# Counting layer 1's softmax sums once a group: pair sums chained by accumulating DMAs in a two-layer graph attention kernel

## The chip, the cores and the metric

The kernel runs on one core of one Trainium2 chip. A core has a matrix engine (TensorE, PE in the profile; its weight loads are the row PEld), VectorE (DVE), ScalarE (ACT), GpSimd (POOL), and SyncE (SP), which here only issues DMAs. Matmuls read SBUF and write PSUM. Each engine runs its own instructions in order and waits on semaphores for the others. The metric is the device time of one execution in microseconds; smaller is better.

## The reference

Sixteen graphs of 1024 nodes with 256 features go through two layers. Each layer normalizes, applies ReLU, runs masked multi-head attention and adds the result to x:

```python
h = maximum(layernorm(x), 0)
q, k, v = h @ Wq, h @ Wk, h @ Wv            # layer 0: 4 heads of 64; layer 1: 8 heads of 32
s = where(adj allows, q @ k.T * scale, -inf)  # per head, 1024 x 1024
out = softmax(s) @ v                        # softmax over the keys
x = x + out @ Wo + bo
```

All of it is in float32. The softmax needs, for every query and head, the sum of the exponentials over all keys.

## The kernel before, in words

**Groups and steps.** Scores are held transposed: keys on the partitions, 512 queries along the free axis. For each batch, layer, half of the queries (qh) and half of the features (g) there is a `Group`: four heads in layer 1, two in layer 0. So there are four groups a layer and batch. A group runs in steps; a step handles four blocks of 128 keys x 512 queries. A layer-1 group has 8 steps (all four heads, one block of keys each), a layer-0 group has 4 (two heads, two blocks of keys each).

**A step.** `scores` issues four matmuls into two PSUM pairs (L372). `exponentials` applies the mask on VectorE with one scalar_tensor_tensor for each half of the step (L388), from PSUM into an SBUF tile p of 128 x 2048 floats, and takes the exponential on ScalarE in place (L393). `weigh` multiplies p with the values and adds into one PSUM bank, po (L405). Three PSUM pairs (`ps_s`) serve the scores and also the projections; po and pz have one bank each.

**The sums.** The sum over keys on the partitions is a matmul with ones (`count`, L278, into pz), four matmuls a count. In layer 1, GpSimd first adds the p tiles of two steps (`count_steps`, L502, 128 x 2048), so there are four counts a group. In layer 0, `add_tiles` adds within a step and along the group on VectorE and GpSimd (L416, L418) and counts once a group.

**The end of a group.** The unnormalized output is copied out of PSUM (L288), the sum is copied (`spread`, L296) and written through DRAM into a compact shape, inverted on VectorE (`invert`, L305), broadcast back through DRAM by DMAs on SP (tile inv), and multiplied in by GpSimd (`normalize`, L324, tile cat). `test` compares the sums with two bounds on GpSimd (L318, L319). After two groups `end_half` multiplies with Wo (L353) and adds to x on VectorE (L358).

**The order.** `Stream.run` walks all steps of all layers: the layer-0 steps of batch b+1 (16, the first of them called `first[b+1]` or a) stand before the layer-1 steps of batch b (32, from `second[b]` or c). At step i it issues scores(i), then the weighing of step i - 2 (LEAD is 2), then the counts that are due, exponentials(i), and the other work that `later` has put down for step i: statistics and norms (`stats`, `norm`, then `add_bias` on GpSimd, L190), transposes of the normalized rows (`turn`, L200), projections (`k`, `q`, L212; `values`, L241), `end_half`, the mask's loads (L126, issued by GpSimd), DMA transposes (`flip`, L130, issued by SP), conversions (`put`, L136, ScalarE) and second passes for layer 1 (`second`, L144, VectorE). At an even step with one of `k`, `q`, `values`, `end_half` the weighing is put off, and the next step weighs two steps at once. The very last group has `hurry`: its last two steps are counted directly, and it ends with `finish`.

**Buffers.** p tiles alternate between tag p0 (even steps, three buffers) and p1 (odd steps, two).

## Time and profile before

| | us |
|---|---|
| median of 3 runs | 3377.39 (3377.24 to 3378.44) |
| the profiled execution | 3380.06 |
| its span, first to last instruction | 3378.3 |
| TensorE (PE) busy | 3339.0 |
| VectorE (DVE) busy | 2501.1 |
| GpSimd (POOL) busy | 2447.1 |
| ScalarE (ACT) busy | 2182.5 |

The granted TensorE clock was 0.998 of full speed. In a row of the groups by line stand the line, engine and operation, what is written and read, the shapes, the number of instructions, then busy time and mean duration in ns, then the idle time of the engine just before them and what ended most of it. In a timeline a row gives the start, the length, the engine, line, operation and the number of instructions merged. In the waits a row gives who waited for whom, the total, the number and the longest. A float32 matmul appears as two instructions in the records, so a count of four matmuls is eight of them.

### The profile page before, as it was taken

Reading aid. Unit: us, or ns where it says so; the run is one execution under the profiler, and the core shown is the slowest. Engines: PE = TensorE matmul, PEld = TensorE weight load, DVE = VectorE, ACT = ScalarE, POOL = GpSimd, SP = SyncE. Lnnn points to the kernel's source line nnn. Section 1 sums busy time; section 2 is a strip of 40 time slices with the busy share of each in tenths; the row PEclk is TensorE's granted clock in tenths of the full one; section 3 lists DMA queues with packets and bytes.
Section 4 is the critical chain, followed back from the end, with each engine's and each line's share of the span. In section 5 each row is a group of like instructions: output and inputs, shape, how many; then the busy total and the mean of one; then the engine's idle time right before and its main releaser. Section 6 shows DMA issues by size and latency. Waiting matters only on the chain. (4 is left out here: it accounts for less than half of the span.)

```text
span 3378.3 us, 46298 instructions
## 1 busy us (share of the span) xinstructions
PE 3339.0 (99%) x18190; PEld 1298.6 (38%) x18190; DVE 2501.1 (74%) x2664; ACT 2182.5 (65%) x2402; POOL 2447.1 (72%) x1606
## 2 busy tenths in 40 slices
PE   8999999999999999999999999999999999999998
PEld 3443333333333333333334333333343333433432
DVE  4676767767677786777867778677786777777876
ACT  5567566675666756667566675666756667665665
POOL 5577778777677766877677686777867778676776
PEclk9999999999999999999999999999999999999999
DMA  6221111212112111121221212212121111210001
GB/s 131 48 42 36 48 39 36 51 36 47 36 36 51 42 42 36 39 48 42 45 39 36 48 39 48 39 39 45 39 47 37 48 39 36 51 38 18 14 17 31
DMA packets 250738, 141.77 MB, mean 42 GB/s; under 512 B 182416, under 2 KB 217488, under 8 KB 250512
## 3 DMA queue, kind: packets, MB, share of 16 engines
q1 hardware_dynamic: 232080, 105.18, 12.6%
q0 software_dynamic: 18432, 33.56, 6.3%
q8 instruction: 144, 2.36, 0.3%
q14 instruction: 82, 0.67, 0.1%
HBM read 120.33 MB, written 18.34 MB: 41 GB/s over the span
## 5 line engine op out<-in xcount | busy, mean ns | idle before, releaser
L393 ACT ACTIVATE p<-p 128x1024 f32<-128x1024 f32 x1536 | 1615.1, 1057 | 973.8 <-DVE p L388 931.7
L388 DVE SCALAR_TENSOR_TENSOR p<-mask,ps 128x1024 f32<-128x1024 fp8e4 x1536 | 1797.0, 1215 | 583.5 <-PE ps L372 553.8
L502 POOL TENSOR_TENSOR p<-p,p 128x2048 f32<-128x2048 f32 x255 | 1161.9, 4557 | 372.2 <-PE po L405 368.3
L372 PE MATMUL ps<-qT,kT 32*128 32x512 f32 (+1 forms) x6144 | 1145.6, 631 | 7.6 <-DVE p L388 4.9
L405 PE MATMUL po<-p,v 128*32 128x512 f32 (+1 forms) x6144 | 992.4, 601 | 0.4 <-ACT o L288 0.4
L418 POOL TENSOR_TENSOR t<-t,t 128x1024 f32<-128x1024 f32 x192 | 486.2, 2532 | 389.8 <-DVE t L416 341.6
L372 PEld LDWEIGHTS ps<-qT,kT 32*128 32x128 f32 (+1 forms) x6144 | 367.7, 184 | 675.7 <-issue 305.3
L405 PEld LDWEIGHTS po<-p,v 128*32 128x32 f32 (+1 forms) x6144 | 227.8, 118 | 689.4 <-issue 529.1
L416 DVE TENSOR_TENSOR t<-p 128x1024 f32<-128x1024 f32 x192 | 325.0, 1693 | 14.6 <-POOL t L418 14.4
L278 PE MATMUL pz<-p,ones 128*32 128x512 f32 x2056 | 267.8, 593 | 0.2 <-POOL p L502 0.2
L212 PE MATMUL pq<-hT,wk 128*128 128x512 f32 x512 | 240.7, 613 | 3.1 <-ACT hT L201 3.1
L353 PE MATMUL py<-wo,cat 128*128 128x256 f32 x1008 | 237.8, 387 | 4.7 <-POOL cat L324 2.8
L241 PE MATMUL pv<-wv,hT 128*128 128x256 f32 x1024 | 237.9, 385 | 0.1
L212 PE MATMUL pq<-hT,wq 128*128 128x512 f32 x512 | 236.6, 605 | 0.0
L241 PEld LDWEIGHTS pv<-wv,hT 128*128 128x128 f32 x1024 | 189.4, 190 | 71.7 <-issue 24.0
L353 PEld LDWEIGHTS py<-wo,cat 128*128 128x128 f32 x1008 | 185.4, 190 | 80.0 <-issue 33.4
L324 POOL TENSOR_TENSOR cat<-o,inv 128x512 f32<-128x512 f32 x127 | 164.5, 1296 | 10.3 <-DMA inv<-vd 9.3
L416 POOL TENSOR_TENSOR t<-p 128x1024 f32<-128x1024 f32 x64 | 165.0, 2578 | 2.8 <-ACT p L393 2.4
L358 DVE TENSOR_TENSOR x<-py,x 128x1024 f32<-128x1024 f32 x63 | 76.4, 1213 | 118.4 <-PE py L353 118.4
L190 POOL TENSOR_TENSOR x<-x,bo 128x1024 f32<-128x1024 f32 x64 | 152.6, 2385 | 1.5 <-DMA bo<-in_bo_dram 1.4
L212 PEld LDWEIGHTS pq<-hT,wk 128*128 128x128 f32 x512 | 93.5, 192 | 145.2 <-issue 120.1
L212 PEld LDWEIGHTS pq<-hT,wq 128*128 128x128 f32 x512 | 92.2, 189 | 139.8 <-issue 138.3
(51 smaller groups left out, 1635.4 us busy)
## 6 DMA issues: line engine op xcount, KB each, us to landing
adj<-in_adj_dram POOLq DMA_DIRECT2D x128, 256.0 KB, 3.6
x<-in_x_dram SPq DMA_DIRECT2D x32, 512.0 KB
inv<-vd SPq DMA_DIRECT2D x128, 128.0 KB
inv<-vd SPq DMA_DIRECT2D x252, 64.0 KB
out_dram<-x SPq DMA_DIRECT2D x31, 512.0 KB
adjT<-adj SPq DMA_TRANSPOSE x128
sd<-s SPq DMA_DIRECT2D x64, 4.0 KB
sn<-sd SPq DMA_DIRECT2D x64, 4.0 KB
```

The costliest lines, as they stand in the source:

```text
L212: nc.tensor.matmul(pq[:, m, :], wt[self.layer][:, c, ts(m, P)], self.hT[half][:, c, :], start=(c == 0), stop=(c == 1),)
L241: nc.tensor.matmul(pv[:, i, :], self.hT[half][:, c, ts(i, P)], w.v[self.layer][:, c, :], start=(c == 0), stop=(c == 1),)
L278: nc.tensor.matmul(self.s[r * self.D : (r + 1) * self.D, :], w.ones[:, : self.D], p[:, r, :], start=start, stop=stop,)
L324: nc.gpsimd.tensor_mul(self.half.cat[:, self.g, :], self.ob, self.inv)
L353: nc.tensor.matmul(py[:, i, :], self.half.cat[:, c, ts(i, P)], w.o[self.layer][:, c, :], start=(c == 0), stop=(c == 1),)
L372: nc.tensor.matmul(st.ps[i // 2][:, i % 2, :], gr.inp.kT[r * D : (r + 1) * D, gr.g, ts(kt, P)], gr.inp.qT[r * D : (r + 1) * D, gr.g, ts(gr ...
L388: nc.vector.scalar_tensor_tensor(out=half, in0=gr.mask.m[:, kt, ts(gr.qh, 512)].unsqueeze(1).to_broadcast([P, 2, 512]), scalar=BIG, in1=st ...
L393: nc.scalar.activation(half, half, AF.Exp, scale=gr.scale)
L405: nc.tensor.matmul(gr.o[r * D : (r + 1) * D, :], gr.inp.v[:, kt, h * D : (h + 1) * D], st.p[:, i, :], start=(kt == 0), stop=(kt == NT - 1),)
L416: engine.tensor_add(t, st.p[:, 0:2, :], st.p[:, 2:4, :])
L418: nc.gpsimd.tensor_add(t, t, gr.t)
L502: nc.gpsimd.tensor_add(one, one, st.p)
```

## The change

Layer 1: the pair sums of a group are no longer counted one by one. They are added to one another by DMAs that accumulate into the destination in SBUF (`accumulate`, issued by GpSimd): pair 0 into pair 1, that into pair 2, that into pair 3, and then the last sum is counted once, eight steps after it was weighed. Groups marked `brief` (the last group of each batch, the last two of the program) accumulate only pair 0 into pair 1 and count three times; the `hurry` group counts as before. The end of a layer-1 group moves from 2, 4, 7 and 9 steps after its last weighing to 8, 10, 12 and 15 (brief: 2, 4, 6, 9), that of a layer-0 group from 2, 3, 5, 7 to 4, 5, 7, 9.

Layer 0: `add_tiles` works on two steps at a time, in place in the p tiles, so the tag t goes. The bias add becomes an accumulating DMA issued by GpSimd. Two small operations of `stats` and the two of `test` move to VectorE. p0 gets seven buffers, adj, adjT and hn one, most small tiles two; q and the mask are kept in halves. The start loads four adjacency tiles at once into p tiles, and the positions of most other work in the order change: two of the large items a batch (an `end_half`, a `values`, a `q` and projections of the next batch move by some steps) now lie in layer 0, 7 there and 9 in layer 1, where it was 5 and 11; the second mask pass moves from layer 0 into layer 1.

```diff
+        def second(self, u):
+            m = self.m[u // 4][:, ts(u % 4, 2), :]
...
-                nc.gpsimd.tensor_scalar_add(ve, mv[:, :, 1], EPS)
+                nc.vector.tensor_scalar_add(ve, mv[:, :, 1], EPS)
...
-                nc.gpsimd.tensor_scalar_mul(less, mv[:, :, 0], -1.0)
+                nc.vector.tensor_scalar_mul(less, mv[:, :, 0], -1.0)
...
-            nc.gpsimd.tensor_add(
-                rows, rows, w.bo[self.layer].unsqueeze(1).to_broadcast([P, 4, E])
+            nc.gpsimd.dma_start(
+                rows, w.bo[self.layer].unsqueeze(1).to_broadcast([P, 4, E]), accum_op=ALU.add
             )
...
+            self.brief = self.last
...
-                ok = small.tile([P, self.n_f], F32, tag="ok", name=f"ok_{self.n}_{op.name}")
-                nc.gpsimd.tensor_scalar(ok, self.sn, bound, 1.0, op0=op, op1=ALU.mult)
-                nc.gpsimd.tensor_mul(c, c, ok)
+                nc.vector.scalar_tensor_tensor(
+                    out=c, in0=self.sn, scalar=bound, in1=c, op0=op, op1=ALU.mult
+                )
...
-        st.p = pp.tile([P, 4, 512], F32, tag=f"p{odd}", bufs=2 if odd else 3, name=f"p_{st.n}")
+        st.p = pp.tile([P, 4, 512], F32, tag=f"p{odd}", bufs=2 if odd else 7, name=f"p_{st.n}")
...
+    def add_tiles(one, two):
+        a, b = one.p[:, 0:2, :], one.p[:, 2:4, :]
+        nc.vector.tensor_add(a, a, b)
+        engine = nc.vector if one.j else nc.gpsimd
+        engine.tensor_add(b, two.p[:, 0:2, :], two.p[:, 2:4, :])
+        nc.gpsimd.tensor_add(a, a, b)
+        if one.j:
+            nc.gpsimd.tensor_add(a, a, one.gr.t)
+        one.gr.t = a
...
+        def accumulate(self, one, two):
+            nc.gpsimd.dma_start(one, two, accum_op=ALU.add)
...
-            else:
+            elif j % 2:
                 one = self.steps[i - LEAD - 1].p
+                if not gr.brief and j == 7:
+                    self.accumulate(gr.two, gr.one)
                 nc.gpsimd.tensor_add(one, one, st.p)
-                self.later(i + 2, gr.count, one, st.j == 1, st.last)
+                if gr.hurry:
+                    self.later(i + 2, gr.count, one, j == 1, False)
+                elif j == 1:
+                    gr.one = one
+                elif j == 3:
+                    self.accumulate(one, gr.one)
+                    gr.one = one
+                    if gr.brief:
+                        self.later(i + 6, gr.count, one, True, False)
+                elif gr.brief:
+                    self.later(i + (4 if j == 5 else 2), gr.count, one, False, st.last)
+                elif j == 5:
+                    gr.two = one
+                else:
+                    self.later(i + 3, self.accumulate, one, gr.two)
+                    self.later(i + 8, gr.count, one, True, True)
...
-                self.later(i + 2, gr.count_added)
-                at = 2, 3, 5, 7
+                self.later(i + 4, gr.count_added)
+                at = 4, 5, 7, 9
             else:
-                at = (2, 3, 4, 8) if gr.last else (2, 4, 7, 9)
+                at = (2, 4, 6, 9) if gr.brief else (8, 10, 12, 15)
...
+    for st in steps[-2 * NT :]:
+        st.gr.brief = True
...
-            norms(mine, 0, a - 10, a - 9, a - 7, a - 6)
-            half_inputs(mine, 0, a - 5, a + 2, a + 4, a + 6)
-            norms(mine, 1, a - 8, a - 7, a - 5, a - 4)
-            half_inputs(mine, 1, a - 3, a + 8, c + 6, c + 4)
-        for kt in range(NT):
-            later(a + 4 + kt, masks[b].second, kt)
+            norms(mine, 0, a - 15, a - 14, a - 12, a - 11)
+            half_inputs(mine, 0, a - 9, a + 2, a + 4, a + 6)
+            norms(mine, 1, a - 11, a - 10, a - 8, a - 7)
+            half_inputs(mine, 1, a - 3, a + 8, c, a + 12)
+        for i, u in zip((2, 4, 8, 10, 12, 16, 20, 26), range(NT)):
+            later(c + i, masks[b + 1].second, u)
...
+                half_inputs(other, 0, c + 1, c + 4, c + 8, c + 12)
+            norms(other, 1, c + 1, c + 2, c + 3, c + 5)
+            half_inputs(other, 1, c + (13 if b == 0 else 7), c + 16, c + 20, c + 26)
+            for i, t in zip((7, 12, 17, 22, 33, 37, 41, 45), range(NT)):
+                later(a + i - 5 + (t > 4), mask.load, t)
+                later(a + i - 2, mask.flip, t)
+                later(a + i, mask.put, t)
```

## The prediction

> **What bounds the kernel now.** I read busy shares and groups by line first, then TensorE's and VectorE's timelines, then waits.
>
> ```profile
> PE 3339.0 (99%) x18190; PEld 1298.6 (38%) x18190; DVE 2501.1 (74%) x2664; ACT 2182.5 (65%) x2402; POOL 2447.1 (72%) x1606
> L502 POOL TENSOR_TENSOR p<-p,p 128x2048 f32<-128x2048 f32 x255 | 1161.9, 4557 | 372.2 <-PE po L405 368.3
> L278 PE MATMUL pz<-p,ones 128*32 128x512 f32 x2056 | 267.8, 593 | 0.2 <-POOL p L502 0.2
> L190 POOL TENSOR_TENSOR x<-x,bo 128x1024 f32<-128x1024 f32 x64 | 152.6, 2385 | 1.5 <-DMA bo<-in_bo_dram 1.4
> adj<-in_adj_dram POOLq DMA_DIRECT2D x128, 256.0 KB, 3.6
> ```
>
> PE reads 99% at granted clock 0.998: matmuls taken off it should shorten the span. The timeline qualifies that (start, length):
>
> ```profile
> 1558.12 1.04 PE L278 MATMUL pz<-p,ones 128*32 128x512 f32 x8
> 1559.09 1.14 PE L372 MATMUL ps<-qT,kT 32*128 32x512 f32 x8
> 1560.17 1.06 PE L405 MATMUL po<-p,v 128*32 128x512 f32 x8
> 1561.16 1.51 PE L372 MATMUL ps<-qT,kT 32*128 32x512 f32 x8
> 1562.61 1.06 PE L405 MATMUL po<-p,v 128*32 128x512 f32 x8
> 1563.49 1.04 PE L278 MATMUL pz<-p,ones 128*32 128x512 f32 x8
> ```
>
> A count (L278) stands 0.97 us before the next scores; a weighing followed by scores has the same 0.10 switch, so a count is worth **0.87**. From starts: layer-1 scores 1.07, weighing 0.99, two together 1.84, a large item (k, q, values, end_half) 3.65, a turn 1.02. The 1.51 is not work: the second scores of a pair wait 0.37 for a PSUM pair. I call a pair of steps heavy with a large item, light without. A light layer-1 pair takes 5.36: 4.12 work, 0.87 count, 0.37 wait. In such pairs VectorE shows
>
> ```profile
> 3257.23 4.62 DVE L388 SCALAR_TENSOR_TENSOR p<-mask,ps 128x1024 f32<-128x1024 fp8e4 x4 [0.75 <-PE ps L372]
> 3262.59 4.62 DVE L388 SCALAR_TENSOR_TENSOR p<-mask,ps 128x1024 f32<-128x1024 fp8e4 x4 [0.74 <-PE ps L372]
> ```
>
> so it idles only 0.75 in 5.36, and GpSimd needs 4.56 for its pair sum (L502). Without the count, light pairs belong to VectorE and GpSimd; only heavy pairs (7.63 of PE work) keep the whole 0.87. The waits already name the next limit:
>
> ```profile
> DVE p L388 <- POOL p L502: 27.6, 16, 2.1
> ```
>
> The 7.6 us of idle that the page gives for L372 hides the stalls inside a row.
>
> **The change, part by part.** *Counts.* Before, 63 layer-1 groups count four times and the last five: 257. After, 47 count once, 16 (the last group of each batch, and the one before the last) three times, the last five times: 100. Off PE: 157 x 0.87 = **-136.6 us**, ten a batch (8.7). By the busy row (99%) all of it would come off the span; by the rows of 1.51 only where VectorE keeps up. The Trainium skill (Perfetto Trace Analysis, Identifying the Most-Contended Engine) speaks against the first reading: matmul busy share is no measure of TensorE's headroom, the weight loads' share (38% here) is nearer.
>
> *Steady batch.* Layer 0 first scores at 344.55 and 3053.43, 13 batches: 208.4 each. PE work before: 8 layer-0 pairs, 5 heavy (11.05) and 3 light (7.56), 77.9; 16 layer-1 pairs, 11 heavy and 5 light, 104.5; 20 counts 17.4, 4 turns 4.1: 204.0, so 4.4 of waits, 2.4 in light pairs (with 0.48 just after one), 2.0 around layer changes. After: 7 heavy and 1 light, 9 heavy and 7 light, 10 counts, 4 turns: 195.2. So two large items move from layer 1, where they gave VectorE time, into layer 0, which is full of PE work already.
>
> *Waits after, in the seven light layer-1 pairs*, by step from the layer's first (c). I follow VectorE in its order: four L388 at 1.16 start 1.18 after the first scores, and a scores' end comes 1.15 after the L388 that frees its PSUM pair (both as at 1559 to 1564). In a bare pair the third L388 ends 1.18 + 3 x 1.16 = 4.66 after the pair's start, so the next pair's scores end at 5.81 where PE alone would have 4.12 + 1.07 = 5.19: 0.62 lost, at c+14. c+6 and c+28 have a turn (1.02 of PE work) as cover: 0.37 and 0.30. c+18 has two stats with aggregates between its L388 (1.08 in the timeline), and behind them ve and less, now on VectorE, 0.15 each by L166 (182 ns, partly overlapped): 0.62 + 1.38 = 2.0. c+22 has the same 1.38 and a turn, and starts late by 0.8 from the stats of c+21: 1.8. c+24: 0.25. c+30: 0.33, the old wait. Sum 5.7.
>
> *GpSimd.* It loses the bias adds (152.6), four test operations a group (136.7) and ve and less (39.2); those go to VectorE, 256 operations at about 0.2 (L305, 219 ns) = 51 us at most, under heavy pairs but for the pieces counted above. It gains 157 accumulating DMAs (10 a batch) and 64 bias DMAs. The issue price is not shown: the nearest row, L126, is 0.62 for 2 KB written a partition; these write 8 and 4 KB. Per row it stays 0.62, by bytes it is 2.47. I take 0.7, the rows being as many. Busy time falls by 328.5 and rises by 221 x 0.7 = 155, to 2270, yet its order matters. From the start of c+18: the sum of pair 18 can start when its even tile is weighed (12.9) and ends at 17.4; the accumulate (0.7), a load (0.6) and cat (1.29) end at 20.0; the rstd pair (1.04 + 0.22) waits for the stats of c+22 anyway and ends near 21.3; the bias issue near 22.0; so the sum of pair 20 ends at 26.5. VectorE wants to write that pair's odd p tile again at 24.3, for c+25: odd tiles still have two buffers, the seven are for even ones. PE would see 1.6 of the 2.2 (its next large item covers the rest); between 0 and 1.6 I take 0.7, since GpSimd's start times are the least sure. Queued behind in GpSimd are the load of c+25, then its transpose on SP and ScalarE's put at c+29, with some 4 us to spare.
>
> *Accumulation time.* 1 MB is 64 KB an engine. Adjacency loads land in 3.6 with 512 KB read; their DMA share gives 6.3% x 3378 / 128 = 1.7 of transfer, so some 2 fixed. One pass at that rate is 3.4, three (read, read, write) 10: 5 to 12 us. Two pair sums (9.1) always stand between the second and third accumulate, about 8 us between the first and second of the third group, and the count comes five steps (over 11 us) after the third; were it late, every matmul behind it would wait, PE being in order. So waits of 0 to 4 us a batch; I take none, since the lower half fits. The Trainium skill (DMA: Bandwidth & Descriptors, Anatomy of one DMA) has about 2 us plus bytes at 436 GB/s: an estimate of 4.4 for 1 MB, under my lower bound, by which the second rival below falls away; no row here shows an accumulate.
>
> *The rest.* q and mask in halves change addresses, not instructions: 0. hn with one buffer: the norm of the next half (c+24) comes after the turn of the first (c+23): 0. Layer-0 sums are four GpSimd and three VectorE adds a group as before, under layer-0 pairs of 11. The second mask pass (0.85) moves from layer 0 into heavy layer-1 pairs, hidden under a 3.65 item, otherwise 0.85 x 8 a batch. Loads and transposes at single buffers are two steps apart or more. The four early loads remove 21.5 us of GpSimd waits (L126 behind adjT) at the start, off the path: 0, between -5 and +3.
>
> *Sum.* Waits after: 5.7 + 0.7 + 2.0 = 8.4 against 4.4. A steady batch gains 8.7 - 4.0 = 4.7 (208.4 to 203.7); 13 give 61. Layer 1 of batch 0: 4.7. Of batch 14, nine light pairs: 4.5. Of batch 15, seven counts (6.1), but group 2 needs on GpSimd 4 x 4.56 + 1.29 + 3 x 0.7 = 21.6 where its four light pairs took 21.4: 4. An end_half falls into the tail, +0.9, beside the last exponentials. Together -61 - 4.7 - 4.5 - 4 + 0.9 = -73. The profiled execution took 3380.1 around a span of 3378.3; the median of the runs is 3377.4, so 3378.3 - 73 = 3305 in the span is **3304** in the runs.
>
> **Rivals.**
> *All of it arrives* (0.16): light pairs shrink as heavy ones do, because work queued on VectorE drains in the heavy pairs: 3377.4 - 137 = 3241. For: VectorE idles 553.8 us for scores. Against: those idle times lie in heavy pairs.
> *Transfers late* (0.14): at 12 us an accumulate, GpSimd stands at the second and third of a group with all pair sums behind it, 3 us more a batch: 3304 + 14 x 3 = 3346.
> *The issue price makes GpSimd the bound* (0.16, slower). In layer 1 it holds 16 sums 72.9, five cat 6.5, three rstd pairs 3.8, five loads 3.1 and 14 issues: 86.3 + 14 Z. Layer 0 now takes 90.6 (84.9 and 6 counts 5.2, with 0.5 waits), so the batch passes 208.4 when layer 1 passes 117.8: Z = 2.25. By bytes (2.47) it is 120.9, 211.5 a batch, +3.1 x 14 = +43: 3420. For: L126's 0.62 may go with bytes. Against: its rows are as many.
> *Counts not fewer* is excluded by the code, but shown by L278.
>
> **How the numbers follow.** Forecast 0.51, alone 3265 to 3345; 0.03 falls within 0.2% (7 us, about what a measurement here can tell). Faster 0.51 + 0.16 + 0.14 = 0.81, same 0.03, slower 0.16. The range 3239 to 3362 takes in the first rival's value and the transfers' bound, not the issue price's.
>
> **What would show it.** L278 p x800 instead of 2056; heavy pairs of 7.63; light ones 4.7 to 7, with scores (L372) lengthened beyond 1.14; waits of L388 for the pair sum well over 27.6 us; accumulate issues near 0.7 and landings under 9. Wrong if layer-1 light pairs run at 4.2, if an issue takes over 2 us, or if GpSimd waits for accumulates.

## The result: 8.2% slower

| | us |
|---|---|
| median of the runs after | 3649.97 (3648.04 to 3665.37) |
| median of the runs before, same chip | 3377.38 (3377.24 to 3378.44) |
| ratio, 95% interval | 1.0816 (1.0787 to 1.0846) |
| profiled execution after, its span | 3650.56, 3648.8 |
| granted TensorE clock after (before) | 0.963 (0.998) |

The busy shares of the page, the groups by line, and the accumulates among the DMA issues (median us to landing last). In these rows L402 is the masked copy, L407 the exponential, L386 the scores, L419 the weighing, L520 the pair sum, L506 the accumulate, L198 the bias DMA, L319 the reciprocal of the inversion, L338 normalize; in some runs a number is off by two. Below, `L319 <- sn` stands for that row of the waits.

```profile
PE 3438.5 (94%) x16934; PEld 1322.2 (36%) x16934; DVE 2721.4 (75%) x3048; ACT 2166.1 (59%) x2402; POOL 2307.4 (63%) x1123
```

```profile
L520 POOL TENSOR_TENSOR p<-p,p 128x2048 f32<-128x2048 f32 x255 | 1194.5, 4688 | 272.3 <-PE po L419 224.0 <-ACT hn L190 24.0 <-ACT p L407 10.4
L331 DVE SCALAR_TENSOR_TENSOR chk<-sn,chk 128x8 f32<-128x8 f32 (+1 forms) x256 | 228.7, 893 | 4.4
L151 DVE TENSOR_SCALAR mask<-mask 128x1024 fp8e4<-128x1024 fp8e4 x128 | 165.6, 1294 | 0.0
L292 PE MATMUL pz<-p,ones 128*32 128x512 f32 (+1 forms) x1056 | 164.8, 595 | 0.0
L506 POOL DMA_DIRECT2D p<-p x157 | 144.9, 923 | 69.3 <-PE po L419 39.0 <-POOL p L520 21.4 <-issue 6.1
L198 POOL DMA_DIRECT2D x<-bo x64 | 92.4, 1453 | 16.4 <-ACT hn L190 9.7 <-DMA bo<-in_bo_dram 5.3 <-issue 0.5
```

```profile
p<-p POOLq DMA_DIRECT2D x157, 1024.0 KB, 7.8
```

The counts did go: L292 has 800 instructions for layer 1 and the unchanged 256 for layer 0. Yet TensorE is busy for 100 us more, with 1256 fewer instructions. Two VectorE groups that the prediction took for small are not: L331 (the test) holds 228.7 us at a mean of 893 ns, though its median is 174, and L151 (second mask pass) 1294 ns where it took 850. The waits:

```profile
DVE vn L319 <- DMA sn<-sd: 162.6, 76, 16.7
POOL cat L338 <- DMA inv<-vd: 160.9, 40, 9.6
ACT o L302 <- POOL cat L338: 124.4, 18, 9.0
ACT mask L143 <- DMA adjT<-adj: 41.2, 13, 14.5
```

Before, the first was 43.5, the second 9.3, and the other two are not in the answer. GpSimd itself hardly waits for an accumulate (0.7 us in all). Where does this fall? I took the start of every step's first masked copy (L402) from the trace. Between layer changes a steady batch now takes 89.4 us in layer 0 (before 84.4) and **135.6 in layer 1 (before 123.7)**; the prediction had 90.6 for layer 0, which leaves 113.1 of its 203.7 for layer 1. In layer 0, TensorE idles 0.3 of the 89.4: it simply holds more work there. Layer 1 holds less work and takes longer. From the start of batch 2 to the start of the last layer, that is 230 of the 270 us between the spans; 22 lie before and 18 after. Two stretches show how. A test beside a pair sum:

```profile
1038.15 4.80 POOL L520 TENSOR_TENSOR p<-p,p 128x2048 f32<-128x2048 f32 x1
1038.19 5.01 DVE L331 SCALAR_TENSOR_TENSOR chk<-sn,chk 128x16 f32<-128x16 f32 x2
...
1043.13 1.22 DVE L402 SCALAR_TENSOR_TENSOR p<-mask,ps 128x1024 f32<-128x1024 fp8e4 x1
```

A test of 128x16 numbers lasts until GpSimd's 4.80 us are over, and the next L402 stands behind it. Of the 256 test instructions, 71 last over 1.5 us (175.9 us together), and all 71 end with a GpSimd tensor_tensor. The second stretch begins with a wait for a pair sum and goes on to one for the sums:

```profile
1913.13 4.62 DVE L402 SCALAR_TENSOR_TENSOR p<-mask,ps 128x1024 f32<-128x1024 fp8e4 x4 [3.90 <-POOL p L520]
...
1924.30 1.13 PE L386 MATMUL ps<-qT,kT 32*128 32x512 f32 x4
...
1926.56 0.25 DVE L319 RECIPROCAL vn<-sn 128x16 f32<-128x16 f32 x1 [3.78 <-DMA sn<-sd]
1926.73 2.29 DVE L402 SCALAR_TENSOR_TENSOR p<-mask,ps 128x1024 f32<-128x1024 fp8e4 x2
...
1927.95 2.08 PE L386 MATMUL ps<-qT,kT 32*128 32x512 f32 x4 [2.53 <-DVE p L402]
...
1929.95 1.94 PE L419 MATMUL po<-p,v 128*32 128x512 f32 x8
```

At c+25 VectorE waits 3.90 us for the odd p tile. At c+27 it stands 3.78 us at the reciprocal because its input is still under way through DRAM; the L402 of the next scores is behind it in order, so TensorE waits 2.53. Then the scores take 2.08 where the same four took 1.13, and a weighing 1.94 instead of 1.06. The windows before, in and after the gap (PEclk is the column behind POOL) say why:

```profile
1907.00:1922.00 15.00, 13.53 (x84) 5.30 (x84) 10.13 (x9) 12.27 (x16) 14.08 (x9) 1.00 1.05 181
1926.00:1934.00 8.00, 6.05 (x24) 2.55 (x26) 7.32 (x7) 3.23 (x4) 6.23 (x3) 0.57 0.94 186
1934.00:1944.00 10.00, 8.87 (x52) 3.74 (x51) 6.97 (x6) 9.08 (x9) 3.42 (x2) 1.00 0.51 105
```

The 0.57 is a mean over the window: the trace's records of the granted clock read 1.0 up to 1926.86, 0.5 from there to 1933.68, and 1.0 again. So this stall costs its own 2.53 us and, TensorE being busy for most of the 6.83 us at half the clock, by estimate some 3 more; a longer "busy" TensorE is in part the slow clock.

### The profile page after: what moved, and what is told of

It reads as the page before. It is cut to its first block, busy times and chain, and to the rows that moved or that the text cites. A ratio compares the mean times of both kernels' runs of the same rounds, so it can differ in the third digit from the quotient of the medians.

```text
span 3648.8 us, 44272 instructions
## 1 busy us (share of the span) xinstructions
PE 3438.5 (94%) x16934; PEld 1322.2 (36%) x16934; DVE 2721.4 (75%) x3048; ACT 2166.1 (59%) x2402; POOL 2307.4 (63%) x1123
## 4 chain that ended last, share of the span: by engine, by line
PE 59%; DVE 16%; DMA 11%; ACT 7%; issue 4%; POOL 3%; SPq 1%; DVEq 0%; POOLq 0%; ACTq 0%
PE ps L386 20%; PE po L419 15%; PE pq L225 11%; DVE p L402 9%; PE py L367 5%; PE pv L253 4%; PE pz L292 3%; ACT p L407 3%; DMA sn<-sd 3%; DMA sd<-s 3%; DMA adjT<-adj 2%; DVE chk L331 2%; DMA inv<-vd 1%; POOL p L520 1%; DVE st L173 1%
## 5 line engine op out<-in xcount | busy, mean ns | idle before, releaser
L407 ACT ACTIVATE p<-p 128x1024 f32<-128x1024 f32 x1536 | 1608.9, 1057 | 1082.3 <-DVE p L402 1044.1
L402 DVE SCALAR_TENSOR_TENSOR p<-mask,ps 128x1024 f32<-128x1024 fp8e4 x1536 | 1796.4, 1214 | 581.0 <-PE ps L386 531.4
L386 PE MATMUL ps<-qT,kT 32*128 32x512 f32 (+1 forms) x6144 | 1312.0, 654 | 145.6 <-DVE p L402 104.3
L520 POOL TENSOR_TENSOR p<-p,p 128x2048 f32<-128x2048 f32 x255 | 1194.5, 4688 | 272.3 <-PE po L419 224.0
L419 PE MATMUL po<-p,v 128*32 128x512 f32 (+1 forms) x6144 | 1020.8, 622 | 1.2 <-ACT o L302 1.2
L386 PEld LDWEIGHTS ps<-qT,kT 32*128 32x128 f32 (+1 forms) x6144 | 411.4, 189 | 930.4 <-issue 367.2
L432 POOL TENSOR_TENSOR p<-p 128x1024 f32<-128x1024 f32 x128 | 303.3, 2369 | 344.8 <-DVE p L431 339.8
L419 PEld LDWEIGHTS po<-p,v 128*32 128x32 f32 (+1 forms) x6144 | 230.4, 119 | 716.5 <-issue 501.6
L431 POOL TENSOR_TENSOR p<-p 128x1024 f32<-128x1024 f32 x64 | 151.3, 2364 | 337.2 <-DVE p L428 98.7
L338 POOL TENSOR_TENSOR cat<-o,inv 128x512 f32<-128x512 f32 x127 | 173.9, 1369 | 166.0 <-DMA inv<-vd 160.9
L331 DVE SCALAR_TENSOR_TENSOR chk<-sn,chk 128x8 f32<-128x8 f32 (+1 forms) x256 | 228.7, 893 | 4.4
L302 ACT COPY o<-po 128x512 f32<-128x512 f32 x128 | 74.1, 579 | 213.0 <-POOL cat L338 124.4
L506 POOL DMA_DIRECT2D p<-p x157 | 144.9, 923 | 69.3 <-PE po L419 39.0
L143 ACT ACTIVATE mask<-adjT,mhalf 128x1024 fp8e4<-128x1024 bf16 x128 | 145.6, 1139 | 41.2 <-DMA adjT<-adj 41.2
L428 DVE TENSOR_TENSOR p<-p 128x1024 f32<-128x1024 f32 x128 | 166.6, 1301 | 0.0
L151 DVE TENSOR_SCALAR mask<-mask 128x1024 fp8e4<-128x1024 fp8e4 x128 | 165.6, 1294 | 0.0
```

Of the source, the lines that this page charges most:

```text
L331: nc.vector.scalar_tensor_tensor(out=c, in0=self.sn, scalar=bound, in1=c, op0=op, op1=ALU.mult)
L338: nc.gpsimd.tensor_mul(self.half.cat[:, self.g, :], self.ob, self.inv)
L386: nc.tensor.matmul(st.ps[i // 2][:, i % 2, :], gr.inp.kT[r * D : (r + 1) * D, gr.g, ts(kt, P)], gr.inp.qT[gr.qh][r * D : (r + 1) * D, gr.g ...
L402: nc.vector.scalar_tensor_tensor(out=half, in0=gr.mask.m[gr.qh][:, kt, :].unsqueeze(1).to_broadcast([P, 2, 512]), scalar=BIG, in1=st.ps[i] ...
L407: nc.scalar.activation(half, half, AF.Exp, scale=gr.scale)
L419: nc.tensor.matmul(gr.o[r * D : (r + 1) * D, :], gr.inp.v[:, kt, h * D : (h + 1) * D], st.p[:, i, :], start=(kt == 0), stop=(kt == NT - 1),)
```

## The experiments

The theories. **A**: the accumulates' megabytes delay other transfers (sums, inv, adjT), and the engines that work in order stand at them. **B**: GpSimd's pair sums hold VectorE in the small operations that were moved there (the test, and `ve` and `less`, the two of `stats`) and in the second mask pass. **C**: copies wait for one of o's two buffers. **D**: the new places of the inputs' work. All ratios are to the kernel before; L0 and L1 are the mean us of a steady batch in the two layers, taken as above.

| run | us | ratio (95%) | clock | L0 | L1 |
|---|---|---|---|---|---|
| before | 3377 | 1 | 0.998 | 84.4 | 123.7 |
| the change | 3650 | 1.0816 (1.0787-1.0846) | 0.963 | 89.4 | 135.6 |
| no_acc | 3553 | 1.0527 (1.0510-1.0545) | 0.978 | 89.2 | 129.2 |
| acc_small | 3604 | 1.0674 (1.0656-1.0692) | 0.967 | 89.3 | 132.5 |
| test_second | 3633 | 1.0772 (1.0747-1.0797) | 0.963 | 89.9 | 134.8 |
| cat2 | 3629 | 1.0748 (1.0727-1.0768) | 0.967 | 89.2 | 134.6 |
| nochain | 3700 | 1.0960 (1.0942-1.0979) | 0.975 | 84.3 | 142.0 |
| old_sched | 3749 | 1.1099 (1.1081-1.1118) | 0.950 | 89.2 | 143.0 |
| all | 3502 | 1.0379 (1.0361-1.0396) | 0.982 | 88.2 | 126.5 |
| cand | 3595 | 1.0645 (1.0621-1.0670) | 0.963 | 86.5 | 135.5 |
| all2 | 3679 | 1.0894 (1.0876-1.0912) | 0.963 | 88.9 | 136.9 |
| all3 | 3695 | 1.0940 (1.0915-1.0964) | 0.960 | 91.0 | 136.5 |
| b_small | 3668 | 1.0861 (1.0843-1.0880) | 0.968 | 85.6 | 140.1 |
| b_bias | 3373 | 0.9986 (0.9977-0.9996) | 0.997 | 83.4 | 123.7 |
| gps | 3563 | 1.0550 (1.0532-1.0567) | 0.970 | 88.7 | 131.2 |
| gps_no_acc | 3494 | 1.0343 (1.0326-1.0360) | 0.979 | 88.8 | 127.4 |
| all4 | 3486 | 1.0324 (1.0307-1.0342) | 0.980 | 89.0 | 124.7 |
| best | 3605 | 1.0671 (1.0643-1.0699) | 0.961 | 94.4 | 127.7 |
| best_no_acc | 3349 | 0.9908 (0.9891-0.9924) | 0.994 | 88.3 | 116.7 |
| best_small | 3387 | 1.0022 (1.0012-1.0031) | 0.989 | 88.3 | 118.9 |

### One cause at a time, taken from the change

**no_acc.**

```diff
         def accumulate(self, one, two):
-            nc.gpsimd.dma_start(one, two, accum_op=ALU.add)
+            return
...
-            nc.scalar.copy(s, self.s)
+            nc.scalar.activation(s, self.s, AF.Identity, bias=w.ones[:, 0:1])
```

> The changed kernel without its 157 accumulating DMAs; each count then sees one pair of a group alone, and 1 is added to the sums when they are copied so that they stay above zero. Theory A (the accumulates' transfers lengthen the round trip of the sums through DRAM, and VectorE, which takes its work in order, stands at the reciprocal L319, GpSimd at cat L338): the wait L319 <- sn falls from 162.6 us to near the 43.5 of before, cat <- inv from 160.9 to near 9, and the time falls by 120 to 220 us, to 3430 to 3530. Theory B (VectorE is held by GpSimd's pair sums in the test L331 and the second mask pass L151): those two keep their 228.7 and 165.6 us, and the time falls by at most what the 144.9 us of issues give GpSimd, under 60 us, to 3590 to 3650.

**acc_small.** With the same second edit:

```diff
-            nc.gpsimd.dma_start(one, two, accum_op=ALU.add)
+            nc.gpsimd.dma_start(one[:, 0, 0:32], two[:, 0, 0:32], accum_op=ALU.add)
```

> The 157 accumulates stay where they are, with the same number of rows, but each row carries 32 of its 2048 numbers (128 bytes of 8192); 1 is added to the sums when they are copied. It separates the bytes moved from the issue (0.92 us each on GpSimd) and from the waits that the chain needs. Theory A: as without accumulates but for the issues, 3440 to 3560. If the issue and the chain's order on GpSimd cost the time, it stays above 3590. Theory B: above 3590 as well.

**test_second.**

```diff
-                nc.vector.scalar_tensor_tensor(
-                    out=c, in0=self.sn, scalar=bound, in1=c, op0=op, op1=ALU.mult
-                )
+                ok = small.tile([P, self.n_f], F32, tag="ok", name=f"ok_{self.n}_{op.name}")
+                nc.gpsimd.tensor_scalar(ok, self.sn, bound, 1.0, op0=op, op1=ALU.mult)
+                nc.gpsimd.tensor_mul(c, c, ok)
...
-        for i, u in zip((2, 4, 8, 10, 12, 16, 20, 26), range(NT)):
-            later(c + i, masks[b + 1].second, u)
+        for u in range(NT):
+            later(a + 4 + u, masks[b].second, u)
...
```

> The changed kernel with the test back on GpSimd as four small operations, and the second mask pass back in layer 0 of the next batch; accumulates as in the change. Theory B: VectorE gets back some 184 us held in the test and 77 in the mask pass, GpSimd takes 137 us of small work again; the time falls by 100 to 220 us, to 3430 to 3550. Theory A: the waits at L319 and at cat stay at about 160 us each and the time falls by less than 60 us, 3590 to 3650, or rises.

**cat2.**

```diff
-            self.ob = work.tile([P, 512], F32, tag="o", name=f"o_{self.n}")
+            if self.g == 0:
+                self.half.cat = work.tile([P, 2, 512], F32, tag="cat", name=f"cat_{self.n}")
+            self.ob = self.half.cat[:, self.g, :]
...
-            nc.gpsimd.tensor_mul(self.half.cat[:, self.g, :], self.ob, self.inv)
+            nc.gpsimd.tensor_mul(self.ob, self.ob, self.inv)
```

> The copies of the weighted values go straight into the tile cat, which gets two buffers instead of one while the two buffers of o go (same memory); normalize works in place. In the change the copy of the first layer-0 group of a batch stands in the same step as the normalize that frees its buffer, so ScalarE waits for GpSimd (L302 <- L338, 124.4 us in 18 waits). Theory C (the two buffers of o are a cause of their own): that wait goes and the time falls by 60 to 120 us, to 3530 to 3590. Theory A: the copy's wait is only what the late inv leaves; PE stands at the same place for VectorE, and the time falls by less than 50 us, to 3600 to 3650.

Against the change's 3650, no_acc gained 97, acc_small 46, test_second 17, cat2 21. no_acc fell between the two ranges; acc_small (A), test_second (B) and cat2 (C) each missed the range of the theory they were to prove and fell in that of the other answer (above 3590, 3590 to 3650, 3600 to 3650). No single cause carries the 273 us. Nor do the waits go as theory A said, to near 43.5 and 9. With no accumulate at all, no_acc still has

```profile
DVE vn L319 <- DMA sn<-sd: 120.5, 66, 4.6
POOL cat L338 <- DMA inv<-vd: 66.3, 39, 4.1
```

So 42 of the 163 us at the reciprocal, and 95 of the 161 at cat, came with the accumulates. Most of the 120.5 stands at the steps a+10, a+14, c+6 and c+27, where the inversion follows one or two steps behind `spread`: there the sums' round trip is short of room, accumulates or not.

In test_second the test is quick again, and VectorE stands elsewhere (and c+8's scores with it):

```profile
1609.90 0.20 DVE L319 RECIPROCAL vn<-sn 128x8 f32<-128x8 f32 x1 [4.39 <-DMA sn<-sd]
...
1611.28 3.18 PE L386 MATMUL ps<-qT,kT 32*128 32x512 f32 x8 [3.70 <-DVE p L402]
...
1614.40 6.12 PE L225 MATMUL pq<-hT,wq 128*128 128x512 f32 x8
```

A wait for sn of 4.39, a TensorE gap of 3.70, and a projection of 6.12 us that takes 3.70 at full clock. The suspicion from here on: the causes cover one another.

### The chain, the places, and all at once

**nochain** puts back the counting of before:

```diff
-                if not gr.brief and j == 7:
-                    self.accumulate(gr.two, gr.one)
                 nc.gpsimd.tensor_add(one, one, st.p)
...
+                self.later(i + 2, gr.count, one, st.j == 1, st.last)
...
-                at = (2, 4, 6, 9) if gr.brief else (8, 10, 12, 15)
+                at = (2, 3, 4, 8) if gr.last else (2, 4, 7, 9)
```

> The changed kernel with the counting of before: each layer-1 pair sum is counted by itself (L278's 2056 matmuls), no accumulating DMA, and the sums leave at the steps of before; all other edits stay. The first runs left 176 of the 273 us unexplained when the accumulates were gone, so a theory D is added: the rest lies in the new places of the inputs' work, in layer 1 above all, where a batch took 135.6 us against 123.7, while layer 0 took 89.4 against 84.4 with TensorE never idle. Theory A with B: without the chain the layer-1 counts cost 137 us again, and the loss by transfers and issues (97 us) goes; 3650 + 137 - 97 - some 60 of counts that fall into waits = 3600 to 3690. Theory D: the layer-1 waits absorb most of the counts; 3500 to 3600. If the chain's dependences themselves (five steps from the last accumulate to the count) were the cause, it would come back near 3380 to 3450.

3700. The waits for the sums are back to before's size (L319 <- sn 41.8 us), so what theory A explains is gone from this kernel (with the accumulates, the layer-1 inversions moved too); the test now holds 315.3 us, so B is not. The time is just above the range of A with B and far from D's.

**old_sched.**

```diff
-            norms(mine, 0, a - 15, a - 14, a - 12, a - 11)
-            half_inputs(mine, 0, a - 9, a + 2, a + 4, a + 6)
-            norms(mine, 1, a - 11, a - 10, a - 8, a - 7)
-            half_inputs(mine, 1, a - 3, a + 8, c, a + 12)
+            norms(mine, 0, a - 10, a - 9, a - 7, a - 6)
+            half_inputs(mine, 0, a - 5, a + 2, a + 4, a + 6)
+            norms(mine, 1, a - 8, a - 7, a - 4, a - 3)
+            half_inputs(mine, 1, a - 3, a + 8, c + 6, c + 4)
...
```

> The changed kernel with chain, bias DMA, test on VectorE and single buffers, but with the inputs' statistics, norms, turns and projections at the steps of before from batch 1 on (one norm a step later, for the single buffer of hn), and the second mask pass in layer 0 of the next batch; the loads of the mask stay at the new steps. Theory D (the placing is the cause): the first pairs of layer 1 (10.9 and 12.1 us, before 8.2 and 5.5) shorten, and the time falls by 120 to 250 us, to 3400 to 3530. Theories A and B: transfers, test and buffers are as in the change; the time falls by less than 60 us (the mask pass alone), 3590 to 3650.

99 us slower than the change, where D wanted 120 to 250 less. Beside the change's other parts the new places of the inputs' work help; D, in this form, falls.

**all** and **cand.** Test, second pass and cat as above, and

```diff
-                at = 4, 5, 7, 9
+                at = (4, 7, 9, 11) if gr.inp.b else (4, 5, 7, 9)
...
-                at = (2, 4, 6, 9) if gr.brief else (8, 10, 12, 15)
+                at = (3, 6, 8, 11) if gr.brief else (8, 12, 14, 17)
+                if gr.inp.b == B - 1 and gr.brief:
+                    at = (2, 4, 6, 9)
...
```

> The changed kernel with the new places of the inputs' work, but with four things undone or relieved together: test on GpSimd, second mask pass in layer 0, the copies straight into a double-buffered cat, and the inversion one or two steps later (loads of x two steps later to suit). Theories A, B and C together: the waits at L319, cat, the test and the copy go, each worth 15 to 100 us; 3400 to 3520. Theory D: the first pairs of layer 1 keep their 10.9 and 12.1 us, and the time stays above 3560.

> The four of the previous kernel and the inputs' work at the steps of before together: only the chain, the bias by DMA, ve and less on VectorE and the single buffers are left of the change. If the theories A to D name all of the causes, it reaches what the prediction expected, 3290 to 3340, and beats both kernels. If something else costs the time (ve and less, the bias DMA's issue of 1.45 us, hn's single buffer), 3400 to 3500.

In these two and in all4 the later end_half of layer 0 comes behind the last batch's layer-1 statistics, which are then taken before the sum is added: the same instructions on other numbers. all is 148 us under the change, in the range of A, B and C together and below what D required (above 3560). cand, with the old places, missed both of its ranges and is slower than all by 93: D falls a second time.

**all2** and **all3.** end_half back on its steps, the inversion one step later; all3 also moves statistics out of the layer change:

```diff
-                at = 4, 5, 7, 9
+                at = 4, 6, 8, 9
...
-            norms(other, 1, c + 1, c + 2, c + 3, c + 5)
+            norms(other, 1, a + 14, a + 15, c + 3, c + 5)
```

> As the kernel with four things undone together (3502 us), but the large items end_half keep the change's own steps: in that run they fell on the steps of k and values, and pairs of 12.3 and 17.2 us stood beside light ones of 5.1 to 6. The inversion is one step later than in the change, no load of x is moved. If the collisions cost what the rows suggest (about 8 us a batch), 3380 to 3440; if only theories A to C count and the collisions are free, 3490 to 3515.

> The previous kernel with one more edit: the statistics of the next batch's second half of x stand at the steps a+14 and a+15 of layer 0 and not at c+1 and c+2, where in the change VectorE is busy for 11.9 of the second layer-1 pair's 12.1 us. If VectorE's pile at the layer change is a cause of its own (theory D in a narrower form), another 30 to 60 us go; if TensorE's own work fills that pair, less than 15 us.

all2 lies 164 us above its higher range, and all3 came out 16 us slower than all2 where it was to gain. I had moved the wait, not taken it away: in layer 0 normalize now stood one step ahead of its end_half, and TensorE itself waited (the row of all2; 119.7 in all3):

```profile
PE py L367 <- POOL cat L338: 123.3, 39, 5.5
```

### The parts put into the kernel before

**b_small** (the change's test, ve and less on VectorE) and **b_bias** (the bias by accumulating DMA), each in the kernel before:

```diff
-                nc.gpsimd.tensor_scalar_add(ve, mv[:, :, 1], EPS)
+                nc.vector.tensor_scalar_add(ve, mv[:, :, 1], EPS)
...
-            nc.gpsimd.tensor_add(
-                rows, rows, w.bo[self.layer].unsqueeze(1).to_broadcast([P, 4, E])
-            )
+            nc.gpsimd.dma_start(
+                rows, w.bo[self.layer].unsqueeze(1).to_broadcast([P, 4, E]), accum_op=ALU.add
+            )
```

> The kernel before with one part of the change alone: test, ve and less on VectorE. Theory B: a test beside a pair sum waits for the sum's end, and the pair's fused mask operations wait behind it; 64 tests of two operations, about half of them against a sum, up to 4.5 us each: 100 to 250 us slower, 3480 to 3630. If the small operations cost what the prediction took (0.2 us each, mostly under heavy pairs), 3370 to 3400.

> The kernel before with the other part alone: the bias of layer outputs added by accumulating DMAs instead of GpSimd's tensor_add. GpSimd gains 64 x (2.39 - 1.45) = 60 us of busy time, which lies beside full TensorE work; 64 transfers of 512 KB share the queues with the sums' round trips. Theory A: those round trips grow, 20 to 80 us slower, 3400 to 3460. Otherwise the same within 10 us, 3367 to 3387.

This is the cleanest result of the study: **the small operations alone cost 290 us**, the bias DMAs gain 4. b_small lies above the range of B, 3480 to 3630, which counted 64 tests where there are 128; b_bias is in the range for no effect. One collision in b_small, and the clock around it:

```profile
1671.84 4.53 POOL L502 TENSOR_TENSOR p<-p,p 128x2048 f32<-128x2048 f32 x1
...
1672.67 3.94 DVE L317 SCALAR_TENSOR_TENSOR chk<-sn,chk 128x16 f32<-128x16 f32 x2
1673.51 1.13 PE L372 MATMUL ps<-qT,kT 32*128 32x512 f32 x4
...
1676.54 2.34 DVE L388 SCALAR_TENSOR_TENSOR p<-mask,ps 128x1024 f32<-128x1024 fp8e4 x2
...
1677.81 2.08 PE L372 MATMUL ps<-qT,kT 32*128 32x512 f32 x4 [3.16 <-DVE p L388]
```

```profile
1676.00:1684.00 8.00, 6.20 (x14) 3.88 (x15) 7.36 (x16) 4.23 (x4) 2.83 (x4) 0.59 0.16 31
```

The test waits for the sum's end (1676.37), L388 starts right behind it, TensorE has lost 3.16 us, and then the clock is 0.5 from 1677.48 to 1684.31 (0.59 is the mean of the window). From the starts of L388, four layer-1 pairs a batch are 4 to 5 us longer than before (c+4, c+22, c+24, c+30), and none of the other twelve by more than 0.3. Those four hold a test or a ve; layer 1 is 16.4 us longer.

### Do the causes cover one another?

**gps** is the change with test, ve, less on GpSimd, the second pass in layer 0 and cat2; **gps_no_acc** also lacks the accumulates.

> The changed kernel with everything that lets GpSimd hold VectorE put back (test, ve and less on GpSimd, the second mask pass in layer 0) and the copies straight into a double-buffered cat; chain, bias DMA and all other places as in the change. Theory B is shown from before's side by 290 us; if it is also what costs the change its time, 3380 to 3450. If the sums' late round trips (theory A) take its place as soon as it is gone, since VectorE then stands at L319 and GpSimd's pair sums come late, 3560 to 3640, with L319 <- sn still at some 160 us.

> The previous kernel without the accumulating DMAs (each count then sees one pair alone, 1 added to the sums as they are copied). If theories A, B and C cover each other, so that each alone gives little (97, 17, 21 us) and together much, 3270 to 3360, near what the prediction had for the changed kernel; if placing costs most, 3430 to 3540.

**all4** is gps with

```diff
-                at = 4, 5, 7, 9
+                at = (4, 7, 10, 13) if gr.inp.b else (4, 5, 7, 9)
...
+                    at = (8, 10, 12, 15) if end else (8, 11, 13, 15)
...
```

> The kernel with GpSimd's small work back and cat doubled, with accumulates, and the inversion later: in layer 0 three steps after the sums leave instead of one, three instead of two in layer 1, with layer 0's end_half four steps later on steps that hold no other large item. If VectorE's wait for the sums is what is left, that wait falls from some 160 us to under 60 and the time to 3350 to 3450; if GpSimd's load in layer 1 is (pair sums late behind issues and small work, L402 <- L520), 3480 to 3580.

gps is 87 us under the change, at the fast end of the range for A taking B's place (L319 <- sn still 135.8 us); all4 is another 77 under it, with that wait at 8.7: the room for the sums' round trip, with accumulates as they were, is worth nearly as much as B and C together. all4 landed where its expectation put GpSimd's load (L402 <- L520, 164.3 us). gps_no_acc, at 3494, was in the range for placing: with B, C and the accumulates gone, 116 us over the kernel before were still unnamed. The room for the round trip is one part (its L319 <- sn is 115.1 us); all4's timeline names another. Between the pair sums that run at c+21 and at c+24 GpSimd issues an accumulate, a load and a bias DMA and does a test, an rstd chain and a cat, 7.35 us in a row, and the odd p tile, of which there are two, comes free late:

```profile
1607.63 4.62 DVE L402 SCALAR_TENSOR_TENSOR p<-mask,ps 128x1024 f32<-128x1024 fp8e4 x4 [6.33 <-POOL p L520]
...
1608.91 2.08 PE L386 MATMUL ps<-qT,kT 32*128 32x512 f32 x4 [3.89 <-DVE p L402]
...
1610.91 5.96 PE L253 MATMUL pv<-wv,hT 128*128 128x256 f32 x16
```

**best, best_no_acc, best_small.** On top of all4 (and with the change's own steps for the last batch):

```diff
+                    at = (8, 11, 13 if gr.qh or gr.g else 17, 15)
...
+            late = gr.layer and not gr.qh and gr.inp.b < B - 1
+            self.later(i + (17 if late else at[1] + 1), gr.test)
...
+            norms(mine, 0, a - 15, a - 14, a - 12, a - 11, bias=a + 1)
+            norms(mine, 1, a - 13, a - 12, a - 8, a - 7, bias=a + 3)
...
+            norms(other, 1, c + 1, c + 2, c + 3, c + 5, bias=c + 37)
```

> The last kernel (GpSimd's small work back, cat doubled, later inversion) with GpSimd's work between the pair sums of c+20 and c+24 thinned: there 7.35 us of issues, test, rstd and cat stood between two sums, VectorE waited 6.33 us for its odd p tile, TensorE 3.89, and the next large item ran 5.96 instead of 3.70. Bias DMAs go into layer 0, the statistics of the second half two steps earlier, test and cat of a layer's first group into c+26. If GpSimd's order in layer 1 is what is left, layer 1 falls from 124.7 to about 116 us and the time from 3486 by 80 to 130 us, to 3355 to 3405; if half-speed stretches stay elsewhere, 3420 to 3480.

> The previous kernel without accumulating DMAs (each count sees one pair alone, 1 added to the sums as they are copied). If issue and transfer of the accumulates still cost time once everything around them is relieved, 30 to 90 us below the previous kernel; if they are hidden then, within 15 us of it. Near 3300 would mean that the prediction's sum was right for a kernel whose waits are covered.

> The kernel with GpSimd's order thinned (3605 us), its accumulates kept in number, place and rows but with 128 bytes a row instead of 8192 (and 1 added to the sums as they are copied). Without accumulates it took 3349. If the bytes are what costs (other transfers, adjT and inv above all, late behind 1 MB of accumulate), nearly all of the 256 us go: 3350 to 3410. If GpSimd's issues (157 x 0.92 us) or the chain's order are, it stays above 3500.

best missed both of its ranges, the higher by 125 us; without accumulates the same kernel takes 3349, 256 below it where 30 to 90 were expected, and with accumulates of 1/64 of the bytes 3387, in the range for the bytes. So in a kernel in which VectorE is not held and GpSimd's order is thinned, **the bytes of the accumulates cost 218 us** (3605 - 3387), and what is left of them, issue and chain together, 38 (3387 - 3349). GpSimd's own wait for the accumulate before, 42.2 us in 18 waits in best (1.9 in best_small), is part of the 218. Where the rest bites:

```profile
POOL cat L338 <- DMA inv<-vd: 112.7, 15, 8.7
ACT mask L143 <- DMA adjT<-adj: 109.1, 23, 8.6
```

```profile
1655.90 0.87 POOL L506 DMA_DIRECT2D p<-p  x1 [2.77 <-DMA p<-p]
1657.09 2.10 SPq L134 DMA_TRANSPOSE adjT<-adj  x1
...
1664.63 1.15 ACT L143 ACTIVATE mask<-adjT,mhalf 128x1024 fp8e4<-128x1024 bf16 x1 [6.75 <-DMA adjT<-adj]
...
1670.08 2.09 PE L386 MATMUL ps<-qT,kT 32*128 32x512 f32 x8 [6.56 <-ACT v L257]
```

The first fence is best's waits, the second its timeline at c+25 to c+28: a transpose issued 1.2 us after an accumulate keeps ScalarE for 6.75 us, the copy of the values comes behind it in order, and TensorE stands 6.56. In best_small the first of the two waits is not in the answer at all and the second is 9.3 us. The loss has no fixed place: what the accumulates made late was inv above all in the change (no_acc), here inv and adjT, whichever stands next to one.

Nothing here beats both kernels by much: b_bias does it by 0.14% (0.04 to 0.23). best_no_acc leaves pair sums out of the counts and is no candidate.

## Why the prediction was wrong, step by step

The forecast was a gain of 73 us, the result a loss of 273. Counts, work and layer 0 came out near what was said; the step that failed is "Waits after", 8.4 us a batch: layer 1 took 22.5 us a batch more than its share of the sum. The bullets take its terms one by one.

- **The counts.** Right in number (800 instructions in layer 1). Their worth could only be seen with the waits covered: best_no_acc, without accumulates and their issues, takes 88.3 + 116.7 = 205.0 a batch, the prediction had 203.7, before 208.1. That fits a sum whose work terms were right; the whole run, 3349, still gains only 29 of the 73 us.
- **"256 operations at about 0.2 (L305, 219 ns) = 51 us at most."** The first step that failed. The tests alone are 256; with `ve` and `less` 384 operations moved. The row the price came from is a reciprocal with one input; in the change the reciprocal, too, stays at 0.2. The test, with two inputs in SBUF, has a median of 174 ns but a mean of 893, since beside a pair sum it lasts to the sum's end. In total the tests hold VectorE for 228.7 us in the change. The price is not the 0.2 us of a row but the time held, the L402 behind it and the clock after: 290 us in b_small. The Trainium skill (SBUF — State Buffer, Who interferes with whom) says that a VectorE instruction with two SBUF inputs contends with a GpSimd instruction that reads SBUF; the 71 long tests agree, and the prediction did not weigh that rule.
- **"The second mask pass (0.85) ... hidden."** It has one input, and took 1294 ns in its new place (before 850). Moving it and the test back gave only 17 us, with A in place; no run moves it alone.
- **"Accumulation time: ... waits of 0 to 4 us a batch; I take none."** For GpSimd and the chain that is what the change's trace shows (0.7 us in total, a landing of 7.8 inside the 5 to 12). The step failed because it asked only who waits for an accumulate, not which other transfers stand behind one: 95 of cat <- inv's 160.9 us and 42 of L319 <- sn's 162.6 go with the accumulates (no_acc). The rival *Transfers late* had the cause, but in the change the wrong waiter, and 42 us; the bytes are worth 46 us in the change as it is (acc_small) and 218 where nothing else covers them (best), GpSimd's own wait included. The estimate of 4.4 us for 1 MB from the Trainium skill (DMA: Bandwidth & Descriptors, Anatomy of one DMA) is short: the accumulate landed in 7.8.
- **No term for the sums' round trip.** The change moves the end of every group, and the sum has no wait for it. Before, L319's counterpart waited 43.5 us for sn, nearly all at c+4. After, 120.5 are left without any accumulate (no_acc) and 115.1 when B and C are undone too (gps_no_acc); with accumulates but a later inversion it is 8.7, and the kernel is 77 us faster (gps to all4).
- **"GpSimd ... between 0 and 1.6 I take 0.7"** at c+24. The place was right, the size not: VectorE waited 3.90 us for L520 there (at c+25) in the batch shown, and the pairs of c+24 and c+26 take 8.1 and 12.8 us. The issue price was part of it: 0.92 and 1.45 us against 0.7, inside the bounds, and far from the 2.25 at which the rival *issue price* would decide. That rival had the right sign by another mechanism.
- **"Sum 5.7", the light pairs.** The bare pair of c+14 takes 5.1, near the 4.7 worked out, and the heavy pairs of c+12 and c+20 take 7.8 and 7.6, as said. The loss sits in pairs next to a collision: c+2 12.1, c+6 9.0, c+26 12.8, c+28 8.8.
- **No term for the clock.** All waits were added at their own length. In the traces the granted clock is either 1.0 or 0.5, and the gaps of 2.53, 3.16 and 3.89 us shown above each ended with the clock at 0.5, for 6.83 us. In the change all 22 TensorE gaps of 2.1 us or more (past the first 60 us, outside a half-clock stretch) saw such a stretch begin before their end or within 3.5 us of it, and 14 of the 24 gaps of 1.2 to 2.1 us. Its trace has 47 of them, 273 us in all, the one before 3 with 17; half of the difference, 128 us, is by estimate the most that they cost. The Trainium skill (TensorE: Matmul & The Clock Gate, What's actually happening) has the halved clock after an idle window of about 3.4 us that runs on its own; here a gap of 2.53 was enough.
- **"hn, adj: 0", and o**, which the prediction did not look at: two buffers of o against a layer-1 normalize that comes five steps later cost 21 us (cat2). No run undoes hn's or adj's single buffer; best_no_acc keeps both, and layer 0's sums in place, and is faster than the kernel before.

Not settled: what share each cause has in the 273 us. A, B and C cover each other (97, 17 and 21 one by one; 164 when B, C and the inversion's room are undone together in all4), so no split is unique. One way down is B and C 87 (gps), then the accumulates 69 (gps_no_acc), then 144 for places alone: the inversion later and GpSimd's order thinned (best_no_acc). With C undone first (cat2 to gps), B is worth 67, not 17.

## What to carry to other kernels

Before moving a small operation to an engine that feeds TensorE, look at what runs beside it and at what is queued behind it: its price is the longest thing it can be held by, not its own row. Before adding a large transfer, list the small ones that other engines wait for in order, and give them room first. When several stalls cover each other, undoing one shows little; put each alone into the good kernel, or take all out and put one back. And when a run without the suspect still shows the wait, ask where the wait stands.

## What the runs showed of the hardware

A VectorE scalar_tensor_tensor of 128x16 numbers beside a GpSimd tensor_tensor took up to 7.07 us (b_small) at a median of 0.18 for all tests. Who starts first decides: in the change all 93 tests over 0.3 us began after the GpSimd instruction that they overlap, and of the 37 short ones that overlap one, 36 began before it. L402, which reads one operand from PSUM, kept its 1215 ns (1214 after). A tensor_scalar of 128x4 (ve) with one input was held too, up to 2.19 us in b_small. An accumulating DMA of 1 MB within SBUF took 0.92 us to issue and 7.8 to land; one of 128x32 numbers 0.89 and 2.1 (acc_small): on GpSimd they cost the same, on the queues they do not.
